# Attention with the softmax sums written by the exponentials, and k's bias on VectorE

## The chip, the cores and the metric

The kernel runs on one core of a Trainium2 chip. The metric is the device time of one execution in microseconds (us). The engines are named as in the profile: PE is TensorE (PEld its weight loads), ACT is ScalarE, DVE is VectorE, POOL is GpSimd, and SP issues the DMAs.

## The reference

Two layers run one after the other on x of shape 128 x 128 x 32 x 32 in float32. The first is attention over the batch at each of the 1024 pixels; the second is a Mamba block, which the change leaves as it is. The first layer, cut to what matters:

```python
xs  = x.reshape(B, C, L).transpose(2, 0, 1)            # L=1024 pixels, B=128, C=128
qkv = xs @ in_proj_weight.T + in_proj_bias
q, k, v = split(qkv, 3);  q = q * hd ** -0.5           # 4 heads of hd=32
scores = einsum('lhbd,lhed->lhbe', q, k)
attn = softmax(scores, axis=-1)                        # rows of 128
out  = einsum('lhbe,lhed->lhbd', attn, v).reshape(L, B, E)
y    = out @ out_proj_weight.T + out_proj_bias + xs
y    = layernorm(y) * norm_weight + norm_bias
```

## The kernel before, in words

`attention_layer` works on groups of four pixels (LG = 4), 256 groups in all; a group's tiles are 128 x 512. The layer's result goes to `mid` in DRAM, from which `mamba_layer` reads afterwards. Channels or batch lie on the partitions.

The work of a group is a list of tasks, each on one engine. `Plan` gives each task a time, its entry in `A_AT` plus the group's number times `A_PERIOD`, sorts the tasks of all groups by that time, and issues them in that order. Each engine so has one fixed queue in which tasks of up to six groups stand between one another, and it takes them strictly in turn. The waits between engines are added from the tiles and the PSUM banks that the instructions touch; the times themselves are in no instruction.

A group's tasks are these, with their lines:

- `picked` (L294, POOL) copies the group's columns of x to `xg`.
- `q_mm`, `k_mm` (L303, PE) project; `q_out` (L322, DVE) adds q's bias and scales by the negative of the scale, `k_out` (L329, ACT) adds k's bias. `v_mm` (L336, PE) and `v_out` (L348, DVE) do v, whose bias is put in later.
- The softmax is made in two halves f = 0, 1 of two pixels each. `scores0/1` (L363, PE) write the half's scores into `s_ps`, which has one PSUM bank for each head; each bank holds all four pixels of its head, so both halves lie in the same four banks. `top0/1` (L394, DVE) take each row's minimum, since the scores are negated. `exps00, exps01, exps10, exps11` (L373, ACT), one for each pixel, are four exponentials of 128 x 128 each, with the row's `top` as a bias read from SBUF.
- `summed0/1` (L385, POOL) add the upper half of each exponentials' row to the lower, twice, from 128 to 32 columns; `inverse0/1` (L410 and L411, DVE) sum these 32 and take the reciprocal; `shares0/1` (L417, DVE) multiply the half's 128 x 1024 exponentials by it.
- For each pixel, `turned0..3` (L435, PE) transpose its four heads, `kept0..3` (L443 on ACT, L441 on DVE for pixel 2) bring them to SBUF, `weighted0..3` (L447, PE) multiply by v. `o_out` (L477, DVE) brings the sum to SBUF.
- `residual` and `projected` (L486, L489, PE), `squared` (L500, ACT), `variance` (L507, PE), `rstd` (L492, L493, ACT) and `normed` (L515, DVE) make the output projection and the layernorm; `placed` (L522, POOL) scales and stores into the tile that SP writes out.

Of the kernel before, what the change touches and what calls it, by code (L numbers as in the profile page):

```python
# [11 lines left out]
AF = mybir.ActivationFunctionType  # L12
ALU = mybir.AluOpType
AX = mybir.AxisListType
# [3 lines left out]
P = 128  # L18
NB = 128
# [8 lines left out]
NH = 4  # L28
# [35 lines left out]
class Plan:  # L64
# [9 lines left out]
    def add(self, *args, **more):  # L74
        t = Task(*args, **more)
        t.image, t.place = self.image, len(self.tasks)
        t.at = t.image * self.period + self.times[t.name]
        deps = list(t.after)
        for k in t.reads:
            if k in self.wrote:  # L80
                deps.append(self.wrote[k])
        for k in t.writes:
            deps += self.read.get(k, ())
            if k in self.wrote:
                deps.append(self.wrote[k])
        for k in t.reads:
            self.read.setdefault(k, []).append(t)
        for k in t.writes:
            self.wrote[k], self.read[k] = t, []
        for x in deps:  # L90
            assert (x.at, x.place) < (t.at, t.place) or x is t, (x.name, t.name)
        self.tasks.append(t)
        return t
# [87 lines left out]
NE = 3  # L181
NET = 6
NSQ = 2
NARROW = 32
EVICT = (2,)
O_DVE = True
PARTS = 12
A_PERIOD = 10.33
A_AT = {
    "exps00": 22.9, "exps01": 21.02, "exps10": 17.58, "exps11": 18.7, "inverse0": 30.84,  # L190
    "inverse1": 25.62, "k_mm": 1.98, "k_out": 3.52, "kept0": 40.48, "kept1": 37.14, "kept2": 41.9,
    "kept3": 41.08, "load": 0.01, "normed": 58.45, "o_out": 48.87, "part": 16.16, "picked": 0.0,
    "placed": 59.65, "projected": 51.66, "q_mm": 6.66, "q_out": 8.24, "residual": 50.11,
    "rstd": 56.14, "scores0": 16.16, "scores1": 14.5, "shares0": 32.27, "shares1": 34.23,
    "squared": 53.2, "store": 59.66, "summed0": 24.57, "summed1": 21.75, "top0": 19.29,
    "top1": 15.91, "turned0": 39.2, "turned1": 35.99, "turned2": 40.75, "turned3": 38.62,
    "v_mm": 31.97, "v_out": 33.54, "variance": 54.6, "weighted0": 45.24, "weighted1": 46.07,
    "weighted2": 46.9, "weighted3": 47.73,
}


# [1 line left out]
def attention_layer(ctx: ExitStack, tc: tile.TileContext, ident, eps, x, w, mid, prepare):  # L203

    nc = tc.nc
# [7 lines left out]
    bqkv = const.tile([P, 3], F32, name="bqkv")  # L213
# [29 lines left out]
    def several(n, shape, name, pool=keep):  # L243
        return [pool.tile(shape, F32, name=f"{name}{j}") for j in range(n)]
# [3 lines left out]
    HL = LG // 2  # L248
# [7 lines left out]
    eTs = several(NET, [P, NH * NB], "eT")  # L256
    oTs = several(2, [P, GB], "oT")
    tops = several(2, [P, HL, NH], "top")
    halves = several(2, [P, HL, NH, NB // 2], "halved")
    sums = several(2, [P, HL, NH], "total")  # L260
    sqs = several(NSQ, [P, GB], "sq")
    s_ps = psum.tile([P, NH, LG, NB], F32, name="s_ps")
    plan = Plan(several(4, [P, GB], "m_ps", psum), A_PERIOD, A_AT)
    add = plan.add
# [5 lines left out]
    def heads(h):  # L270
        return slice(h * HD, (h + 1) * HD)
# [13 lines left out]
    def group(g):  # L285
        plan.image = g
        xg, qT, kT, v = xgs[g % NXG], qTs[g % NQK], kTs[g % NQK], vs[g % NV]
# [7 lines left out]
            writes=[kx],  # L295
        )

        def project(j, name, engine, move, key):
# [26 lines left out]
        project(  # L325
            1,
            "k",
            "ACT",
            lambda b: nc.scalar.activation(kT, b, AF.Identity, bias=bqkv[:, 1:2]),  # L329
            kk,  # L330
        )
        bank = Bank()
# [1 line left out]
        def v_mm(bank=bank):  # L334
# [14 lines left out]
            writes=[kv],  # L349
# [3 lines left out]

        def softmax(f):
            e, ke = es[f][g % NE], f"e{f}{g % NE}"
            ls = slice(f * HL, (f + 1) * HL)
            got = s_ps[:, :, ls, :].rearrange("p h l k -> p l h k")

            def scores():
                for i in range(f * HL, (f + 1) * HL):  # L360
                    cs = slice(i * NB, (i + 1) * NB)
                    for h in range(NH):
                        nc.tensor.matmul(  # L363
                            s_ps[:, h, i, :],
                            lhsT=qT[heads(h), cs],
                            rhs=kT[heads(h), cs],
                            start=True,
                            stop=True,
                        )

            def exps(i):
                for h in range(NH):
                    nc.scalar.activation(  # L373
                        e[:, i, h, :],
                        s_ps[:, h, f * HL + i, :],
                        AF.Exp,
                        bias=tops[f][:, i, h : h + 1],
                        scale=-1.0,
                    )

            def summed():
                src, w = e, NB // 2
                while w >= NARROW:
                    dst = halves[f][:, :, :, 0:w]
                    nc.gpsimd.tensor_tensor(  # L385
                        dst, src[:, :, :, 0:w], src[:, :, :, w : 2 * w], ALU.add
                    )
                    src, w = dst, w // 2

            add(f"scores{f}", "PE", scores, reads=[kq, kk], writes=[f"s{f}0", f"s{f}1"])  # L390
            add(
                f"top{f}",
                "DVE",
                lambda: nc.vector.tensor_reduce(tops[f], got, AX.X, ALU.min),  # L394
                reads=[f"s{f}0", f"s{f}1"],
                writes=[f"top{f}"],
            )
            for i in range(HL):
                add(
                    f"exps{f}{i}",  # L400
                    "ACT",
                    lambda i=i: exps(i),
                    reads=[f"s{f}{i}", f"top{f}"],
                    writes=[f"{ke}{i}"],
                )
            both = [f"{ke}{i}" for i in range(HL)]
            add(f"summed{f}", "POOL", summed, reads=both, writes=[f"half{f}"])

            def inverse():
                nc.vector.reduce_sum(sums[f], halves[f][:, :, :, 0:NARROW], AX.X)  # L410
                nc.vector.reciprocal(sums[f], sums[f])  # L411

            add(f"inverse{f}", "DVE", inverse, reads=[f"half{f}"], writes=[f"sum{f}"])
            add(
                f"shares{f}",
                "DVE",
                lambda: nc.vector.tensor_tensor(  # L417
                    e, e, sums[f].unsqueeze(3).to_broadcast([P, HL, NH, NB]), ALU.mult
                ),
                reads=[f"sum{f}"],  # L420
                writes=both,
            )

        for f in range(2):
            softmax(f)

        pv = Bank()
        for i in range(LG):
            f = i // HL
# [15 lines left out]
            def weighted(i=i, r=r):  # L445
# [16 lines left out]
                writes=[f"eT{r}"],  # L462
# [7 lines left out]
                reads=[f"eT{r}", kv],  # L470
# [4 lines left out]
            "o_out",  # L475
            "DVE" if O_DVE else "ACT",
            lambda: (nc.vector.tensor_copy if O_DVE else nc.scalar.copy)(oT, pv.tile),  # L477
            writes=[ko],
# [12 lines left out]
        def rstd():  # L491
# [9 lines left out]
            writes=[kz],  # L501
# [6 lines left out]
            reads=[kz],  # L508
# [7 lines left out]
            writes=[kz],  # L516
# [13 lines left out]
            reads=[kz],  # L530
# [10 lines left out]
    for g in range(NT):  # L541
        if g % PER == 0:
            b = g // PER
            plan.image = g - PER - 1 if b else -2
            if plan.image < 0:
                plan.image = b - 3
            add("load", "SP", lambda b=b: load(b))
        group(g)
        if 4 <= g < 4 + PARTS:
            add("part", "PE", prepare_part, take=[spare], give=[spare])  # L550
        if g % PER == PER - 1:
            add("store", "SP", lambda b=g // PER: store(b))
# [984 lines left out]
@with_exitstack  # L1537
def both_layers(ctx: ExitStack, tc: tile.TileContext, x, w, out):
    nc = tc.nc
    const = ctx.enter_context(tc.tile_pool(name="const", bufs=1))  # L1540
    dram = ctx.enter_context(
        tc.tile_pool(name="dram", bufs=1, space=bass.MemoryType.DRAM)
    )
    ident = const.tile([P, P], F32, name="ident")
    make_identity(nc, ident)
    eps = const.tile([P, 1], F32, name="eps")
    nc.vector.memset(eps, LN_EPS)
    mid = dram.tile([NB, P, L], F32, name="mid")
    b_const = ctx.enter_context(tc.tile_pool(name="b_const", bufs=1))
    with tc.tile_pool(name="b_prep", bufs=1) as prep:  # L1550
        constants = attention_layer(
            tc,
            ident,
            eps,
            x,
            w,
            mid,
            lambda bank: mamba_constants(tc, ident, eps, w, b_const, prep, bank),
        )
    mamba_layer(tc, ident, eps, mid, constants, out)  # L1560
# [50 lines left out]
```

## Time and profile before

| | |
|---|---|
| median of 3 runs | 15083.57 us (15081.0 to 15085.92) |
| the profiled execution | 15083.06 us, its span 15081.2 us |
| busy shares of the span | PE 88%, DVE 94%, ACT 82%, POOL 91% |
| attention layer | from the start to about 2888 us; 256 groups |
| a group in the steady state | about 10.97 us |
| granted TensorE clock, steady attention | 1.00 |

A group of instructions is read as: line, engine, operation, output and input tiles, shapes and count; then the busy time in us and the mean duration of one in ns; then the engine's idle time ahead of it and who ended that. In the timeline each row has the start in us, the length in us, then the instruction and, in brackets, the idle time just before it with its releaser.

### The profile page before, as it was taken

How to read it: one execution, taken by the hardware profiler on the slowest of the kernel's cores; microseconds unless marked ns; L12 is line 12 of the kernel's file. 1: busy time of each engine (PE TensorE's matmuls, PEld its weight loads, DVE VectorE, ACT ScalarE, POOL GpSimd, SP SyncE). 2: the span in 40 equal slices, each digit the busy share in tenths (PEclk: the TensorE clock that was granted, in tenths of full speed). 3: DMA queues.
4: the chain of work that ended last, by engine and by line, in shares of the span. 5: the costliest groups of instructions: out<-in, count | busy, mean ns of one | idle time of the engine just before them, and what ended most of it. 6: DMA issues, size and time to landing. Idle time of an engine off the chain costs nothing. (4 is left out here: it accounts for less than half of the span.)

```text
span 15081.2 us, 218873 instructions
## 1 busy us (share of the span) xinstructions
PE 13259.9 (88%) x78902; PEld 6352.1 (42%) x78902; DVE 14172.1 (94%) x9777; ACT 12324.6 (82%) x22790; POOL 13799.0 (91%) x5385
## 2 busy tenths in 40 slices
PE   8999999888888888888888888888888888888887
PEld 4555555433333333333333333333333333333333
DVE  7888888699999999999999999999999999999999
ACT  6777777688888888888888888888888888888887
POOL 6777777599999999999999999999999999999999
PEclk9999999999999999999999999999999999999999
DMA  2222222266666666666666666666666666666665
GB/s 50 57 46 51 52 46 46 56 168 169 168 169 168 168 170 169 169 169 169 168 169 169 169 169 169 169 169 169 168 169 170 168 169 168 168 169 169 170 168 146
DMA packets 1191586, 2180.31 MB, mean 145 GB/s; under 512 B 673232, under 2 KB 674272, under 8 KB 1190496
## 3 DMA queue, kind: packets, MB, share of 16 engines
q1 hardware_dynamic: 1190496, 2166.31, 59.5%
q8 instruction: 619, 10.14, 0.3%
q14 instruction: 471, 3.86, 0.1%
HBM read 1746.30 MB, written 419.43 MB: 144 GB/s over the span
## 5 line engine op out<-in xcount | busy, mean ns | idle before, releaser
L1338 POOL TENSOR_TENSOR dbu<-dtxr,brep 128x2048 f32<-128x2048 f32 x1280 | 5804.1, 4551 | 26.3 <-DMA dtxr<-dtxd 13.1
L1384 POOL TENSOR_TENSOR hc<-hc,crep 128x1024 f32<-128x1024 f32 x2304 | 5412.4, 2373 | 307.4 <-PE da L1331 205.3
L1363 ACT ACTIVATE da<-dtr,aneg 128x1024 f32<-128x1024 f32 x2560 | 2951.2, 1161 | 524.3 <-DVE hc L1384 502.1
L1376 DVE TENSOR_TENSOR_SCAN hc<-da,dbu 128x1024 f32<-128x1024 f32 x1408 | 3161.8, 2276 | 98.0 <-ACT da L1363 91.9
L1277 ACT ACTIVATE bx<-p_ps,bT 128x128 f32<-128x128 f32 (+1 forms) x8192 | 2791.4, 484 | 132.1 <-PE p_ps L1269 132.1
L1376 DVE TENSOR_TENSOR_SCAN da<-da,dbu 128x1024 f32<-128x1024 f32 x1152 | 2621.9, 2286 | 101.9 <-ACT da L1363 93.9
L1331 PE MATMUL da<-ident,bx 128*128 128x128 f32 x12288 | 1827.7, 294 | 501.8 <-DVE hc L1376 418.7
L1384 DVE TENSOR_TENSOR hc<-da,crep 128x1024 f32<-128x1024 f32 x1792 | 2161.8, 1218 | 47.8 <-PE y_ps L1403 7.5
L891 PE MATMUL p_ps<-tn,wk 128*128 128x512 f32 x4096 | 1987.3, 608 | 249.3 <-DVE tn L855 156.5
L1331 PEld LDWEIGHTS da<-ident,bx 128*128 128x128 f32 x12288 | 1488.4, 150 | 1635.4 <-DVE hc L1376 1074.0
L1363 ACT ACTIVATE dbu<-dtr,aneg 128x1024 f32<-128x1024 f32 x1536 | 1731.9, 1217 | 452.9 <-DMA dtr<-dtd 449.9
L1376 DVE TENSOR_TENSOR_SCAN hc<-dbu,da 128x1024 f32<-128x1024 f32 x896 | 1999.4, 2267 | 27.5 <-ACT dbu L1363 24.2
L1403 PE MATMUL y_ps<-hc,fold 128*32 128x512 f32 x16384 | 1972.9, 599 | 43.3 <-POOL hc L1384 30.4
L1376 DVE TENSOR_TENSOR_SCAN da<-dbu,da 128x1024 f32<-128x1024 f32 x640 | 1449.7, 2281 | 188.8 <-PE da L1331 126.4
L373 ACT ACTIVATE e<-s_ps,top 128x128 f32<-128x128 f32 x4096 | 1147.7, 384 | 338.4 <-PE s_ps L363 299.1
L952 PE MATMUL p_ps<-xpad,dwd 64*64 64x512 f32 x9216 | 1154.4, 593 | 111.0 <-ACT xm L923 103.6
L891 PEld LDWEIGHTS p_ps<-tn,wk 128*128 128x128 f32 x4096 | 709.9, 191 | 1148.8 <-issue 774.5
L1403 PEld LDWEIGHTS y_ps<-hc,fold 128*32 128x32 f32 x16384 | 475.5, 109 | 1188.6 <-issue 846.0
L385 POOL TENSOR_TENSOR halved<-e 128x512 f32<-128x512 f32 x512 | 916.3, 1790 | 25.6 <-ACT e L373 19.8
L417 DVE TENSOR_TENSOR e<-e,total 128x1024 f32<-128x1024 f32 x512 | 833.1, 1627 | 0.0
L294 POOL COPY xg<-xt 128x512 f32<-128x512 f32 x256 | 273.6, 1069 | 533.1 <-PE m_ps L486 496.6
L952 PEld LDWEIGHTS p_ps<-xpad,dwd 64*64 64x64 f32 x9216 | 362.6, 133 | 801.3 <-issue 569.2
(128 smaller groups left out, 19118.0 us busy)
## 6 DMA issues: line engine op xcount, KB each, us to landing
dtxr<-dtxd SPq DMA_DIRECT2D x2048, 256.0 KB, 5.4
dtr<-dtd SPq DMA_DIRECT2D x2048, 256.0 KB, 5.4
crep<-bcd SPq DMA_DIRECT2D x2048, 128.0 KB, 6.3
brep<-bcd SPq DMA_DIRECT2D x1536, 128.0 KB, 4.9
x<-mid SPq DMA_DIRECT2D x256, 512.0 KB, 5.5
dtd<-dtt SPq DMA_DIRECT2D x256, 512.0 KB, 5.1
dtxd<-dtt SPq DMA_DIRECT2D x256, 512.0 KB, 4.3
xt<-in_x SPq DMA_DIRECT2D x64, 1024.0 KB, 11.0
```

Of the source, the lines that this page charges most:

```text
L373: nc.scalar.activation(e[:, i, h, :], s_ps[:, h, f * HL + i, :], AF.Exp, bias=tops[f][:, i, h : h + 1], scale=-1.0,)
L385: nc.gpsimd.tensor_tensor(dst, src[:, :, :, 0:w], src[:, :, :, w : 2 * w], ALU.add)
L417: lambda: nc.vector.tensor_tensor(e, e, sums[f].unsqueeze(3).to_broadcast([P, HL, NH, NB]), ALU.mult),
L891: nc.tensor.matmul(a.tile, lhsT=wk[:, k, h * P : (h + 1) * P], rhs=tn[:, c * CH + k : (c + 1) * CH + k], start=k == 0, stop=c > 0 and k == ...
L952: nc.tensor.matmul(pair[r] .tile[c * HP : (c + 1) * HP] .rearrange("p (r q) -> p r q", q=HH), lhsT=dwd[rs, k, :], rhs=xpad[rs, y0 : y0 + r ...
L1277: nc.scalar.activation(bx[:, tb, ks, n, :], src, AF.Copy, scale=bT[:, j : j + 1])
L1331: nc.tensor.transpose(ps[:, tb * P : (tb + 1) * P], bx[:, tb, TENSOR[h, nb] * NDB + db].rearrange("p n d -> p (n d)"), ident,)
L1338: nc.gpsimd.tensor_mul(dbu[u // 2 % NDBU], dtxr[db // 2], brep[nb - 1].unsqueeze(1).to_broadcast([P, 2, L]),)
L1363: lambda: nc.scalar.activation(a, dtr[db // 2][:, db % 2, :], AF.Exp, scale=aneg[:, h * NDB + db, nb : nb + 1],),
L1376: lambda: nc.vector.tensor_tensor_scan(dst, a, b, 0.0, ALU.mult, ALU.add),
L1384: lambda: engine.tensor_mul(hc[u % 8], dst, crep[nb]),
L1403: nc.tensor.matmul(y_ps[db * GD : (db + 1) * GD, chunk(c)], lhsT=fold, rhs=hc[(i * NG + k) % 8][:, chunk(c)], start=False, stop=last,)
```

## The change

Each exponential now also has `accum_out`, which writes the sum of its row into `total`; the sums have three buffers for each half instead of one. The two POOL additions of each half and the DVE reduction are gone, and the reciprocal stands at the head of `shares`. `k_out` moves from ACT to DVE, as an addition with the bias read from SBUF. The times in `A_AT`, and so the order of every engine's queue, are new; `A_PERIOD` stays 10.33.

```diff
-NARROW = 32
+K_DVE = True
 A_AT = {
...
-    halves = several(2, [P, HL, NH, NB // 2], "halved")
-    sums = several(2, [P, HL, NH], "total")
+    sums = [several(NE, [P, HL, NH], f"total{f}_") for f in range(2)]
...
             "k",
-            "ACT",
-            lambda b: nc.scalar.activation(kT, b, AF.Identity, bias=bqkv[:, 1:2]),
+            "DVE" if K_DVE else "ACT",
+            lambda b: (
+                nc.vector.tensor_scalar(kT, b, bqkv[:, 1:2], None, ALU.add)
+                if K_DVE
+                else nc.scalar.activation(kT, b, AF.Identity, bias=bqkv[:, 1:2])
+            ),
...
                         bias=tops[f][:, i, h : h + 1],
                         scale=-1.0,
+                        accum_out=total[:, i, h : h + 1],
...
-            def summed():
-                src, w = e, NB // 2
-                while w >= NARROW:
-                    dst = halves[f][:, :, :, 0:w]
-                    nc.gpsimd.tensor_tensor(
-                        dst, src[:, :, :, 0:w], src[:, :, :, w : 2 * w], ALU.add
-                    )
-                    src, w = dst, w // 2
...
-            def inverse():
-                nc.vector.reduce_sum(sums[f], halves[f][:, :, :, 0:NARROW], AX.X)
-                nc.vector.reciprocal(sums[f], sums[f])
...
+            def shares():
+                nc.vector.reciprocal(total, total)
+                nc.vector.tensor_tensor(
+                    e, e, total.unsqueeze(3).to_broadcast([P, HL, NH, NB]), ALU.mult
+                )
```

In the steady state the queues of the two programs stand as follows (a group's worth, by task names):

| engine | before | after |
|---|---|---|
| ACT | exps01, squared, exps00, k_out, rstd, kept1, exps10, exps11, kept0, kept3 | exps00, kept0, kept1, exps01, kept3, squared, exps10, exps11, rstd |
| DVE | shares0, v_out, shares1, inverse1, top1, normed, o_out, q_out, top0, inverse0, kept2 | top1, shares0, v_out, q_out, top0, o_out, k_out, normed, shares1, kept2 |
| POOL | summed0, summed1, placed, picked | placed, picked |
| PE | k_mm, variance, weighted, scores1, weighted, turned, weighted, scores0, weighted, q_mm, turned twice, residual, turned, projected, v_mm | weighted, projected, v_mm, weighted, q_mm, scores0, weighted, variance, weighted, k_mm, scores1, turned twice, residual, turned twice |

## The prediction

> **What bounds it now.** First the busy shares, then two stretches of the attention layer, where the whole change lies.
>
> ```profile
> PE 13259.9 (88%) x78902; PEld 6352.1 (42%) x78902; DVE 14172.1 (94%) x9777; ACT 12324.6 (82%) x22790; POOL 13799.0 (91%) x5385
> ```
>
> ```profile
> 600.00:900.00 300.00, 278.02 (x2668) 165.75 (x2666) 269.40 (x357) 234.04 (x632) 222.00 (x165) 1.00 0.22 43
> 2400.00:2700.00 300.00, 278.02 (x2666) 165.70 (x2665) 269.40 (x357) 234.01 (x632) 222.24 (x165) 1.00 0.16 29
> ```
>
> The page's shares mix two layers; the windows (length, then busy PE, PEld, DVE, ACT, POOL, then the clock) show attention as a machine that repeats itself: PE 93%, DVE 90%, ACT 78%, POOL 74%, clock 1.00. No engine is full. One group takes 10.97 us (the same row in the timeline comes back 10.97 later), so something goes round in a circle of waits. The timeline of one group shows it:
>
> ```profile
> 1500.19 1.23 DVE L394 TENSOR_REDUCE top<-s_ps 128x8 f32<-128x1024 f32 x1
> 1500.24 1.07 ACT L443 COPY eT<-m_ps 128x512 f32<-128x512 f32 x2
> ...
> 1501.45 1.14 ACT L373 ACTIVATE e<-s_ps,top 128x128 f32<-128x128 f32 x4
> ...
> 1502.17 1.25 POOL L385 TENSOR_TENSOR halved<-e 128x512 f32<-128x512 f32 x1
> ...
> 1502.46 2.06 DVE L417 TENSOR_TENSOR e<-e,total 128x1024 f32<-128x1024 f32 x1
> ...
> 1505.04 1.21 DVE L417 TENSOR_TENSOR e<-e,total 128x1024 f32<-128x1024 f32 x1
> ...
> 1506.92 1.18 DVE L394 TENSOR_REDUCE top<-s_ps 128x8 f32<-128x1024 f32 x1
> ...
> 1508.03 0.74 DVE L515 SCALAR_TENSOR_TENSOR sq<-m_ps,by,sq 128x512 f32<-128x512 f32 x1
> ...
> 1508.16 0.73 PE L363 MATMUL s_ps<-kT,qT 32*128 32x128 f32 x16 [0.61 <-DVE top L394]
> ...
> 1508.88 1.24 POOL L522 TENSOR_SCALAR yt<-sq,nw,nb 128x512 f32<-128x512 f32 x1 [0.70 <-DVE sq L515]
> 1508.96 2.18 ACT L373 ACTIVATE e<-s_ps,top 128x128 f32<-128x128 f32 x8 [1.14 <-PE s_ps L363]
> ...
> 1510.34 0.75 DVE L322 TENSOR_SCALAR qT<-m_ps,bqkv 128x512 f32<-128x512 f32 x1 [0.34 <-PE m_ps L303]
> ```
>
> DVE works without a gap from one q_out to the end of top1 (1499.37, one period before 1510.34, to 1508.10: 8.73 us). Then PE does scores0, weighted and q_mm until q_out can start at 1510.34: 2.24. Together 10.97, the period. Two things inside it matter. The first `shares` takes 2.06 where the second takes 1.21: a POOL addition had started 0.29 earlier. And the eight exponentials wait for scores0 (1508.16 to 1508.89), though they read the other half: both halves lie in the same banks, and PE, DVE and ACT take these banks in turn.
>
> **Part by part.** *POOL additions* (L385, 4 for each group): POOL keeps picked and placed, 2.3 us of 10.97. POOL is not in the circle, so its own time is worth nothing; what counts is that shares0 falls from 2.06 to 1.21, -0.85. *Reductions* (L410, 0.41 each): two leave DVE, -0.66 by start-to-start (0.41 less the 0.08 by which DVE's successors overlap). *k's bias*: ACT loses 0.69 (L329); DVE gains an instruction like q_out, 0.75 less 0.08 = +0.67. kT is read by the scores of its group some 7 us later, so a late k_out costs nothing beyond its place in DVE's queue. DVE's sum so falls by about 0.84; the old circle would take 10.13 by that, but its order is gone and a new one must be looked for.
>
> *Reads of the sums.* The built program has 4096 instructions on ACT of a kind that was not there, one for each exponential; I take them for the reads of the sums. No row shows one. Call x what each adds. Its neighbours, from ACT's timeline in the second layer and at the start:
>
> ```profile
> 5031.58 0.27 ACT L1167 COPY bT<-p_ps 128x32 f32<-128x32 f32 x2 [0.76 <-PE p_ps L1162]
> ```
>
> ```profile
> 88.86 0.20 ACT L619 ACTIVATE bns<-bns 128x1 f32<-128x1 f32 x1
> ```
>
> Two small copies, one right behind the other, take 0.27; one alone is 0.189 (L1167's median), so the second costs 0.08. Consecutive exponentials start 0.25 apart though each lasts 0.38: they overlap by 0.13. A read that must see its exponential finished loses that, and the 128x1 row standing alone takes 0.20: at worst 0.33. At best 0, if it hides behind the next one's fetch of its bias; below 0 is excluded, since an instruction more in a queue taken in turn shortens nothing. I take 0.09, nearest to the small copy that follows its like, a little over because it needs its predecessor's result.
>
> *The Trainium skill's price.* "ScalarE: Activation LUTs", section "What ACT_TABLE_LOAD costs", gives 186 ns plus 0.833 per element and an overlap of 93, so a one-element instruction would be about 94 ns as an estimate; no row here has it.
>
> **What goes round after.** In the new order ACT does exps10, then PE scores0 (which waits for ACT), then ACT exps11 (which waits for PE), then DVE top0 (waits for ACT), and every turn changes engine. (These waits stand in the built program; the banks again, and top0's place behind exps11.) Handovers are from the timeline above: DVE to PE 0.05 (1508.10, 1508.16), PE to ACT 0.07 (1508.89, 1508.96), DVE to ACT 0.03 (1501.42, 1501.45), ACT to DVE 0.03 (the last exponential ahead of 1500.19 ends at 1500.16). ACT to PE has no row; 0.05, between the others. Four exponentials in a row are 1.15 (1.14 to 1.17).
>
> Circle B, the banks alone: top1 1.18+.03, exps10 1.15+.05, scores0 0.73+.07, exps11 1.15+.03, top0 1.23+.05, scores1 0.73+.07, then exps00, kept0, kept1, exps01 in ACT's queue 1.02+0.48+0.48+1.15, and .03 back to top1: 9.63, and 16 reads: 9.63+16x.
>
> Circle A leaves ACT at top0 and goes on along DVE's queue: top1 through exps11 as above 4.39 with 8 reads; top0 1.15, o_out 0.61, k_out 0.67, normed 0.66, reciprocal 0.24, shares1 1.13, kept2 0.56 (each from its start to the next one's, so its length less 0.08; the reciprocal's 0.24 has the 0.04 that L417 waits for it): 9.41+8x. But shares1 now stands behind normed, and placed, which normed releases on POOL, starts 0.11 after normed's end (1508.88 against 1508.77), shares1 0.16 after. If the POOL instruction that came first holds up the multiplication as the addition did (0.96 of it was left, 0.85 was lost), 1.19 is left here and 1.08 is lost: 10.49+8x. Bounds 0 and 1.08; below 0 is excluded, since shares1 at 1.13 is the free row. I take 1.08: it is the same DVE instruction, and POOL is first by 0.05.
>
> *A rule against the change here.* "SBUF — State Buffer", section "Who interferes with whom", says that a VectorE instruction with two SBUF inputs contends with a GpSimd one that reads SBUF, whichever starts first holding it to its end. Row and rule meet for additions; for a one-input POOL instruction no row shows it. By the rule circle A is 10.49+8x; were it only for additions, 9.41+8x.
>
> PE alone needs 0.927 of 10.97 = 10.17, a floor.
>
> **Sum.** x = 0.09: A 11.21, B 11.07. A sets the period: +0.24 on 256 groups = +61 us. The profiled execution took 15083.06 (span 15081.2 and 1.9 around it), 0.5 below the median: 15145. Break-even is x = 0.06 for A, 0.084 for B; so k's bias, 0.67 in A, and the reductions saved are both small against the order of turns and 8 or 16 reads. If A loses its collision, B is next at 11.07 (+26 us); the sign stays.
>
> **Rivals.** (1) *The read hides*: x at 0.055, which is the small copy's 0.08 without its 32 columns (0.83 ns each: a 512-column copy costs 0.48 behind its like, 1.07 for the two at 1500.24 less 0.59 for one). A 10.93 with the collision: -10 us; B 10.51 where shares1 goes first: -118 us, 14965. At x = 0 without collision PE's floor decides, 10.17: -205 us, 14878. For: ACT overlaps small instructions, 22% of ACT is idle, POOL gets out of DVE's way. Against: the circle has no slack, so each tenth of a us in x is 0.8 or 1.6 in the period. It decides below x = 0.06. (2) *The read waits for its exponential's end*: x = 0.20, B 12.83, +476 us, 15559; at 0.33, 14.91, +1009 us. For: rstd's second instruction, which needs the first's result, starts only 0.03 after its end, without overlap. Against: the sum is formed inside ACT, not read from memory, so no such wait need arise; no row tells. (3) *No reads*: the sums come free with the exponentials, x = 0; then it is rival 1's end. The extra instructions speak against it.
>
> **Numbers.** Forecast (x 0.07 to 0.13) 0.45; read hidden 0.35, of which most is faster and a part within 0.2%; read waiting 0.20. A measurement of this kernel tells about 0.2%, 30 us, from no change. Faster 0.30, same 0.12, slower 0.58. The range goes from rival 1 without collision (14960) to B at x = 0.18 (12.51, +394, and some for rival 2: 15500); out of it stay a hidden read at PE's floor, 0.07, and the waiting read's far end, 0.12.
>
> **What would show it.** Right: the period in the timeline near 11.2; four exponentials lasting about 1.5 with their reads; shares0 1.21, shares1 above 2 with placed starting just ahead of it; scores0 released by ACT; busy shares of about 91% for PE (10.17 of 11.21), 83% for ACT (8.58 less 0.69, 1.44 more), 30% for POOL, and DVE near its 90%, since the collision gives back what it saved. Wrong: reads of 0.05 or less between exponentials, shares1 at 1.21, or PE above 95% with ACT idle. If x is over 0.15, DVE waits long ahead of both tops, and ACT is the fullest engine.

## The result: 0.28% slower, by a circle through the score banks

The changed kernel takes 15124.22 us (median of ten, 15115.99 to 15131.28) against 15083.62 for the kernel before on the same chip, a ratio of 1.0028 (95% interval 1.0018 to 1.0037): 40.6 us more. The profiled execution has a span of 15118.3 us. A group now takes 11.126 us in the steady state, where it took 10.974; 0.152 more on 256 groups is 39 us. In the traces the last placed ends at 2887.6 us before and at 2925.4 after, 37.8 later, and the spans differ by 37.1, so the whole difference lies in the attention layer.

The window of the changed kernel that answers to the ones of before (length, then busy PE, PEld, DVE, ACT, POOL, the clock):

```profile
600.00:900.00 300.00, 289.86 (x2642) 161.59 (x2645) 239.75 (x325) 248.38 (x1026) 87.03 (x54) 1.00 0.22 43
```

VectorE fell from 90% to 80%, GpSimd from 74% to 29%, ScalarE rose from 78% to 83%: the change did take its work off the two engines it meant to relieve, and the kernel got slower. PE, at 97%, seems nearly full; run 1 below shows its own work in this order to be 10.61 of the 11.13.

The profile page's groups of the exponentials show how each of them now leaves two rows:

```profile
L376 ACT ACTIVATE e<-s_ps,top 128x128 f32<-128x128 f32 x4096 | 1457.9, 377 | 537.7 <-PE s_ps L366 476.7
...
L376 ACT ACTIVATION_READ_ACCUMULATOR e<-s_ps,top 128x1 f32 x4096 | 878.6, 215 | 0.0
```

The read of the sum is an instruction of its own, 0.215 us long. In the rows from 1501.25 on below, it starts before its exponential has ended (1501.51 against 1501.62), and the next exponential (1501.61) before the read has ended (1501.70), so its length is not its price: exponentials that follow one another start 0.250 us apart before (median of 3331) and 0.342 after, so a read costs 0.092.

The timeline of one group shows the circle. It is read by the brackets: each turn waits for the engine that had the banks last.

```profile
1500.45 0.73 PE L366 MATMUL s_ps<-kT,qT 32*128 32x128 f32 x16 [0.32 <-ACT e L376]
...
1501.25 0.37 ACT L376 ACTIVATE e<-s_ps,top 128x128 f32<-128x128 f32 x1 [0.85 <-PE s_ps L366]
...
1501.51 0.19 ACT L376 ACTIVATION_READ_ACCUMULATOR e<-s_ps,top 128x1 f32 x1
1501.61 0.36 ACT L376 ACTIVATE e<-s_ps,top 128x128 f32<-128x128 f32 x1
...
1502.78 1.23 DVE L389 TENSOR_REDUCE top<-s_ps 128x8 f32<-128x1024 f32 x1 [1.29 <-ACT e L376]
...
1504.06 0.54 PEld L366 LDWEIGHTS s_ps<-kT,qT 32*128 32x128 f32 x16 [0.89 <-DVE top L389]
1504.06 0.73 PE L366 MATMUL s_ps<-kT,qT 32*128 32x128 f32 x16
...
1504.86 0.37 ACT L376 ACTIVATE e<-s_ps,top 128x128 f32<-128x128 f32 x1 [0.82 <-PE s_ps L366]
...
1506.02 2.30 POOL L514 TENSOR_SCALAR yt<-sq,nw,nb 128x512 f32<-128x512 f32 x1 [7.90 <-DVE total L404]
1506.07 1.23 DVE L405 TENSOR_TENSOR e<-e,total 128x1024 f32<-128x1024 f32 x1
...
1508.47 0.26 ACT L376 ACTIVATION_READ_ACCUMULATOR e<-s_ps,top 128x1 f32 x1
...
1508.76 1.23 DVE L389 TENSOR_REDUCE top<-s_ps 128x8 f32<-128x1024 f32 x1 [0.87 <-ACT e L376]
...
1510.02 0.37 ACT L376 ACTIVATE e<-s_ps,top 128x128 f32<-128x128 f32 x1 [0.23 <-DVE top L389]
1510.13 1.22 DVE L405 TENSOR_TENSOR e<-e,total 128x1024 f32<-128x1024 f32 x1
```

scores0 (1500.45) waits for ACT's exps10, exps11 (1501.25) waits for PE, top0 (1502.78) for ACT, scores1 (1504.06, by its weight load) for DVE, exps00 (1504.86) for PE; two copies and exps01 run on to 1508.73, top1 (1508.76) waits for ACT, and the next exps10 (1510.02) for top1. At each of these turns the next engine starts within 0.07 us of the end of the one before. Where the three engines stand idle is seen in the list of waits between 1000 and 2033 us (total, times, longest), some 93 groups:

```profile
DVE top L389 <- ACT e L376: 201.2, 186, 1.3
ACT e L376 <- PE s_ps L366: 155.0, 186, 0.8
PEld s_ps L366 <- ACT e L376: 105.2, 92, 1.1
PEld s_ps L366 <- DVE top L389: 82.6, 93, 0.9
```

VectorE alone stands 2.2 us of each group waiting for exponentials. By this circle a relief of VectorE can't help, and whatever makes one of ScalarE's turns longer counts in full; runs 1 to 3 test it.

### The profile page after: what moved, and what is told of

Read it like the earlier page. It is cut to its first block, busy times and chain, and to the rows that moved or that the text cites. A ratio compares the mean times of both kernels' runs of the same rounds, so it can differ in the third digit from the quotient of the medians.

```text
span 15118.3 us, 221409 instructions
## 1 busy us (share of the span) xinstructions
PE 13405.2 (89%) x78902; PEld 6336.0 (42%) x78902; DVE 13936.1 (92%) x9521; ACT 12488.0 (83%) x26630; POOL 12544.5 (83%) x4361
## 3 DMA queue, kind: packets, MB, share of 16 engines
q8 instruction: 619, 10.14, 0.3%
## 5 line engine op out<-in xcount | busy, mean ns | idle before, releaser
L514 POOL TENSOR_SCALAR yt<-sq,nw,nb 128x512 f32<-128x512 f32 x256 | 585.7, 2288 | 2025.4 <-DVE total L404 1988.0
L376 ACT ACTIVATE e<-s_ps,top 128x128 f32<-128x128 f32 x4096 | 1457.9, 377 | 537.7 <-PE s_ps L366 476.7
L389 DVE TENSOR_REDUCE top<-s_ps 128x8 f32<-128x1024 f32 x512 | 627.1, 1225 | 545.6 <-ACT e L376 545.6
L376 ACT ACTIVATION_READ_ACCUMULATOR e<-s_ps,top 128x1 f32 x4096 | 878.6, 215 | 0.0
L1139 POOL TENSOR_TENSOR dtt<-dtt,xm 128x1024 f32<-128x1024 f32 x256 | 608.0, 2375 | 108.1 <-DMA dtd<-dtt 101.9
```

The lines of the kernel that those rows point to most:

```text
L376: nc.scalar.activation(e[:, i, h, :], s_ps[:, h, f * HL + i, :], AF.Exp, bias=tops[f][:, i, h : h + 1], scale=-1.0, accum_out=total[:, i, ...
L1139: lambda: nc.gpsimd.tensor_mul(dtt[h], dtt[h], im["xm"][h]),
```

## The experiments

Each comparison is with the kernel before on the same chip, which took 15099.62 us in the first four runs and 15088.38 in the second four. Against these, the changed kernel's 1.0028 stands for 15142 and 15131 us.

**1. No reads.** The exponentials write no sums, and `total` is set to 1 once.

```diff
+    for one in sums[0] + sums[1]:
+        nc.vector.memset(one, 1.0)
...
-                        accum_out=total[:, i, h : h + 1],
```

> The changed kernel without accum_out: the row sums are left out (each is held at 1), all else as in the changed kernel, the timetable too. Theory, the circle through the score banks: the period is 9.63 plus 16 reads of 0.093; without the reads the banks need 9.63, VectorE's queue 9.41, and PE's own work (about 10.2 to 10.4) sets the period, so 14890 to 14940 us, and PE is over 95% busy. Rival, the reads are hidden and the new order alone made the kernel slower: within 10 us of 15124.

Measured: 15002.04 us, ratio 0.9933 (0.9918 to 0.9948), the group 10.61 us. The window:

```profile
600.00:900.00 300.00, 300.00 (x2781) 169.31 (x2779) 255.87 (x339) 219.68 (x622) 90.26 (x56) 1.00 0.29 56
```

The reads cost 0.52 us for each group, 132 us by the period and 140 by the times: they are not hidden, and the rival falls. But the 98 us gained against before fall some 45 us short of the least that the theory gave. PE has not one gap (300.00 of 300.00). The ends of its rows are modelled, but the distances between its starts say the same: they are those of run 6, where one product alone waits for another engine. So PE's own work in this order is 10.61, not 10.2 to 10.4. What makes it so is tried in 7.

**2. Reads in one half.** `accum_out` is left out for f = 1, whose sums are held at 1.

```diff
+    for one in sums[1]:
+        nc.vector.memset(one, 1.0)
...
-                        accum_out=total[:, i, h : h + 1],
+                        accum_out=total[:, i, h : h + 1] if f == 0 else None,
```

> accum_out in the first half alone; the second half's row sums are left out (held at 1). Theory: 9.63 plus 8 reads of 0.093 is 10.38, near PE's own work, so 14925 to 14960 us. Rival, reads hidden: 15124. If each read cost twice as much where it ends a turn on the banks, 4 of them counting, it would be halfway between the others.

Measured: 15012.15 us, ratio 0.9941 (0.9924 to 0.9958), the group 10.63, PE again without a gap. Eight reads cost almost nothing (0.02 over none) and the other eight 0.50. That is what a circle of 9.63 plus 0.093 for each read gives beside PE's 10.61: 10.38 with eight, under it; 11.12 with sixteen, over it. The time came out some 35 us over the range given, again for PE's share.

**3. k's bias back on ScalarE**, in the new order.

```diff
-K_DVE = True
+K_DVE = False
```

> The changed kernel with k's bias back on ScalarE, at the same place in the timetable (ahead of exps00). Theory: on ScalarE k_out falls into the 0.8 us that it waits there for scores1, and VectorE's queue is not in the circle, so the period stays 11.13 and the time 15115 to 15135 us. Rival, VectorE's queue with normed, the multiplication and k_out sets the period: 0.67 less for each group, 14950 us.

Measured: 15138.74 us, ratio 1.0025 (1.0015 to 1.0035), the group 11.125 as with the change. VectorE is at 75% here and ScalarE at 89%, and nothing moves: neither queue is the bound, and this part of the change is worth nothing in this order.

**4. The sums by the exponentials, in the order of before.** All times of `A_AT` are before's (those of the tasks that are gone stand unused), and k's bias is on ScalarE.

```diff
-K_DVE = True
+K_DVE = False
...
 A_AT = {
-    "exps00": 17.78, "exps01": 20.59, "exps10": 23.43, "exps11": 24.93, "k_mm": 5.93,
...
+    "exps00": 22.9, "exps01": 21.02, "exps10": 17.58, "exps11": 18.7, "inverse0": 30.84,
...
```

> The sums by accum_out, but k's bias on ScalarE and every time from the table of before (so the old order without the POOL additions and VectorE's reductions). Theory, what counts is how often the turn on the banks changes engine and what stands between: in the old order the eight exponentials of the second half follow one another and only squared stands between the other two fours, so about 10.5 to 10.65 and 14965 to 15005 us, faster than before. Rival, 16 reads cost 1.5 in any order: the old circle's 10.97 less 0.85 and 0.66 plus 1.5 is 10.96, 15080 us.

Measured: 15022.69 us, ratio 0.9947 (0.9932 to 0.9962), the group 10.68, just over the 10.65 that was given. So the sums on ScalarE, all sixteen reads of them, make the kernel faster by 77 us in the old order. It is the new order that loses that and more: run 3, which differs from this one in the order alone, is 116 us slower. In the old order the eight exponentials of the second half stand in one run, and PE goes on with other work meanwhile; it waits about 0.2 for the banks here, by its starts.

**5. k's bias on VectorE, in the order of before**: run 4 with `K_DVE = True`.

> The sums by accum_out under the old times, and k's bias on VectorE as in the change, at its old time. Against the run with it on ScalarE (period 10.67) this tells what that part is worth: VectorE gets 0.67 more, and waits 0.3 to 0.5 ahead of three of its instructions, so it is partly hidden: 10.67 to 10.85, 15022 to 15070 us on a chip where the kernel before takes 15100. If VectorE's queue is in that circle in full, 11.3 and slower than before.

Measured: 15025.06 us, ratio 0.9960 (0.9946 to 0.9974), the group 10.74. The intervals of 4 and 5 overlap; by the periods this part costs 0.06 on each group, 15 us, of the 0.67 that VectorE gets. That its waits (2.2 us of each group in run 4) cover the rest is the likely reason, not a shown one.

**6. Shorter turns.** From the changed kernel, the two copies that stand between exps00 and exps01 go to VectorE, and two instructions move in their queues.

```diff
-EVICT = (2,)
+EVICT = (0, 1, 2)
...
-    "scores0": 14.21, "scores1": 17.23, "shares0": 22.86, "shares1": 29.43, "squared": 53.73,
+    "scores0": 14.21, "scores1": 17.23, "shares0": 22.86, "shares1": 35.7, "squared": 55.2,
```

> The changed kernel with kept0 and kept1 on VectorE (EVICT 0, 1, 2), shares1 moved in VectorE's queue to the wait ahead of top0, and squared moved behind exps10 in ScalarE's. All 16 reads stay. Theory, the circle through the banks: it loses the two copies between exps00 and exps01, 9.63 less 0.96 plus 16 reads is 10.17, below PE's own 10.61 in this order, so 10.61 to 10.7 and 14990 to 15025 us on a chip where the kernel before takes 15100, the same as without reads. Rival, reads cost their time on ScalarE wherever they stand: 11.1, 15140 there. Rival, VectorE with three more instructions becomes the bound: over 10.8.

Measured: 15031.17 us, ratio 0.9962 (0.9947 to 0.9977), the group 10.74, PE busy 298.32 of 300. With all the reads in place and VectorE loaded from 80% to 95%, the kernel is 0.39 us faster for each group than the changed one. The rivals of 11.1 and of VectorE as the bound fall. The period came out 0.04 over the range given: PE, though all but full, waits 0.13 of it ahead of scores1 for top0. Which circle makes it wait is seen in 7.

**7. PE's order.** In addition, weighted1 and weighted2 are moved next to weighted0 and weighted3.

```diff
-    "weighted0": 41.76, "weighted1": 43.98, "weighted2": 45.78, "weighted3": 47.0,
+    "weighted0": 41.76, "weighted1": 41.9, "weighted2": 46.9, "weighted3": 47.0,
```

> As the version with short turns, and weighted1 next to weighted0, weighted2 next to weighted3 in PE's queue, so that four fewer times PE goes between full 128-row products and the narrow ones of heads. If the 0.1 us that a 512-column product takes more next to a narrow one (1.13 against 1.02) is what makes PE's own time 10.61, PE needs about 10.2 to 10.25, the banks 10.17, and the period is 10.2 to 10.35: 14905 to 14945 us on a chip where the kernel before takes 15100. If these 0.1 are only a matter of how ends are drawn in the records, it stays at 10.61, 15010 us.

Measured: 14952.63 us, ratio 0.9909 (0.9894 to 0.9924), the group 10.405. This beats both kernels, by 136 us and about 178. The window, with VectorE and PE both at 98%:

```profile
600.00:900.00 300.00, 294.49 (x2829) 174.90 (x2826) 294.78 (x405) 235.81 (x1043) 63.70 (x58) 1.00 0.30 58
```

So PE's order is worth real time, and its starts show where. From scores1 to the next scores0 PE goes through its queue without a wait in both runs, in 7.13 us in run 6 and in 6.80 here; this 0.33 is the whole gain. Two weighted in one run take 0.57 from start to start instead of twice 0.36 (0.14 less), and v_mm and q_mm, each with a narrow neighbour less, are followed 0.09 and 0.10 sooner. The other pair of weighted, between scores0 and scores1, saves as much, but there PE only waits longer for top0. (PE goes between full and narrow products 8 times for each group here and 10 times in run 6; "four fewer" was miscounted.)

What a narrow neighbour costs a 512-column product is seen in the run without reads. Two of its rows, each with the one behind it, are:

```profile
1503.27 1.13 PE L500 MATMUL m_ps<-sq,a_mean 128*128 128x512 f32 x2
1504.32 0.42 PE L440 MATMUL m_ps<-eT,v 128*32 128x128 f32 x8
...
1507.32 1.02 PE L479 MATMUL m_ps<-xg,resc 128*128 128x512 f32 x2
1508.18 1.04 PE L428 MATMUL m_ps<-ident,e 128*128 128x128 f32 x8
```

Between narrow products the next instruction starts 1.05 after a 512-column one, between full ones 0.86, so each narrow neighbour costs it about 0.1. "TensorEngine Tiling (Array Packing)" in the Trainium skill, section "Key Properties", says that changing the tiling mode drains the engine. These rows agree with a cost at each change; that a drain is what costs, they don't tell.

The group came out 0.05 over the upper end that I gave, and the trace shows what keeps it there, a third circle:

```profile
1501.02 0.73 PE L366 MATMUL s_ps<-kT,qT 32*128 32x128 f32 x16
...
1501.81 0.37 ACT L376 ACTIVATE e<-s_ps,top 128x128 f32<-128x128 f32 x1 [0.53 <-PE s_ps L366]
...
1503.10 0.21 ACT L376 ACTIVATION_READ_ACCUMULATOR e<-s_ps,top 128x1 f32 x1
...
1503.35 1.23 DVE L389 TENSOR_REDUCE top<-s_ps 128x8 f32<-128x1024 f32 x1
...
1504.63 0.73 PE L366 MATMUL s_ps<-kT,qT 32*128 32x128 f32 x16 [0.20 <-DVE top L389]
...
1511.42 0.73 PE L366 MATMUL s_ps<-kT,qT 32*128 32x128 f32 x16
```

From scores0 (1501.02) the banks go to exps11, to top0, which starts 0.04 behind the last read, and back to PE for scores1 (1504.63): 3.61. Then PE's queue leads to the next scores0: 6.80. Together they are 10.41, and with run 6's 7.13 they are 10.74, its period. So in both runs PE's queue and one round of the banks set the period, and neither PE's own work nor VectorE's queue alone; four of the sixteen reads still lie in that round.

**8. Who holds whom up, GpSimd or VectorE.** In VectorE's queue normed goes ahead of k_out, so that placed starts well ahead of shares1.

```diff
-    "normed": 59.67, "o_out": 47.67, "part": 14.21, "picked": 0.0, "placed": 60.72,
+    "normed": 58.9, "o_out": 47.67, "part": 14.21, "picked": 0.0, "placed": 60.72,
```

> The changed kernel with normed ahead of k_out in VectorE's queue, so that placed starts on POOL about 0.7 us ahead of shares1 instead of 0.04. If the instruction that starts first keeps the other waiting, placed takes 1.24 as alone and shares1 is held up by about 0.5, to 1.65 to 1.75. If VectorE's multiplication goes first against a POOL instruction with one input whenever they meet, shares1 stays at 1.22 and placed grows to about 2.3. The period stays 11.13 either way, since VectorE's queue has 0.87 to spare ahead of top1: 15115 to 15140 us by the times of the first runs.

Measured: 15128.42 us, ratio 1.0029 (1.0018 to 1.0040), the group 11.126, as expected. The timeline:

```profile
1504.50 1.24 POOL L514 TENSOR_SCALAR yt<-sq,nw,nb 128x512 f32<-128x512 f32 x1 [8.05 <-DVE sq L507]
...
1505.20 1.43 DVE L405 TENSOR_TENSOR e<-e,total 128x1024 f32<-128x1024 f32 x1
...
1505.95 1.63 POOL L292 COPY xg<-xt 128x512 f32<-128x512 f32 x1 [0.21 <-PE m_ps L478]
```

placed, first by 0.70, takes its 1.24, and shares1 loses 0.21; the copy that starts behind shares1 takes 1.63 instead of 1.06. So the two hold each other up also where GpSimd has one input, the row that was missing, and the one that is clearly first goes on. But shares1 lost only 0.21 of the 0.54 that placed still had by its row, where I expected 0.5. "SBUF — State Buffer" in the Trainium skill, section "Who interferes with whom", calls the ports that the two share an exclusive lock; a hold to the recorded end of placed is more than this row shows.

## Why the prediction was right, and where it was not

- **The sign and the size.** 15145 was forecast, 15124 measured: +61 against +41 us. The range held it. That the sum came within 21 us is in part luck: it was the sum of circle A, which does not bound, as said below.
- **The price of a read.** 0.09 was taken, 0.092 is measured; it lies by the small copy that follows its like, far from the bound of 0.33. Rival 2, a read that waits for its exponential's end, falls. The estimate of 94 ns from "ScalarE: Activation LUTs" in the Trainium skill ("What ACT_TABLE_LOAD costs"), which no row of before had, agrees with these 92.
- **Circle B.** 9.63 + 16 x 0.093 is 11.12; measured 11.126. Its terms hold but for hundredths: exps00 to the end of exps01 3.87 (3.13 and eight reads are 3.87), four exponentials with their reads 1.50 (for 1.52), the handover from ACT to PE, of which there was no row, 0.05; top1 took 1.23 and not 1.18.
- **The step that failed: circle A's collision.** I had placed start first, hold up shares1 by 1.08, and so make A the longer circle at 11.21. In the trace placed does start first, by 0.04 (median of 189), but shares1 takes 1.23, as shares0 does with GpSimd idle, and placed is the one that is held up, to 2.30. A is then 9.41 + 8 x 0.093 = 10.15 and bounds nothing. Run 8 fits with a row of GpSimd that begins before and ends after the time in which it holds VectorE up, so that 0.04 between two starts would not decide; what exactly is held when, no run tells. (In the kernel before, the one addition that started 0.06 ahead of a multiplication did hold it up, to 2.29.) The sum stayed near because B stood just below A; for a lost collision +26 us was given. The measured +41 is B with a read of 0.092 to 0.093 instead of 0.09 (8 to 12 us more), and the hundredths of the other terms.
- **PE's floor.** 10.17 was PE's busy share of before, taken as if it went with the work alone. It goes with the order: 10.61 in the new one (run 1), and 10.14 by PE's starts, its wait left out, in run 7's. So rival 1's prices were too good: with a read that costs nothing the gain is 98 us, not 205, and not 118. PE's busy share, forecast at 91%, is 97% for that reason.
- **Busy shares.** ScalarE is at 83% as forecast; VectorE at 80% and not 90, since the collision did not fall on it. GpSimd's 29% meets the forecast 30 by luck: the two instructions that it keeps, 2.3 us by the prediction's own figure, would be 21% of 11.21, and it is at 29% because placed was the one held up, to 2.30.
- **k's bias.** Said to be small; shown as nothing in the new order; about 15 us in the old one, by the periods.

What the change lost is thus shown: not by the sums on ScalarE, which gain 77 us in the old order, but by an order in which ScalarE, PE and VectorE take the score banks in turn so that ScalarE has three turns in a group, two of four exponentials and one of eight with two copies between them, and the reads on top. Taking the circle apart, with banks of its own for each half, was not tried.

## What to carry to other kernels

When no engine is full, look for what all of them take in turn (here four banks that hold both halves of the scores) and sum the circle around it, handovers included: an instruction added inside costs in full, one taken from an engine outside it is worth nothing, until the next circle or a full engine is reached. An instruction's price is what it adds between the starts of its neighbours, not its length. A busy share of another order is no floor: what PE needs depends on what stands next to what.

## What the runs showed of the hardware that I had not expected

- A 512-column float32 product (two rows in the trace) takes 1.13 us behind products of 32 rows or 32 columns and 1.02 behind full ones; with narrow ones on both sides it costs 0.2 us more from start to start. Sixteen narrow products in one run take 0.57 where two runs of eight take 0.71. Moving two tasks to join such runs gave 0.33 us for each group.
- A GpSimd instruction whose row starts 0.04 us ahead of that of VectorE's multiplication was held up by it for 1.06 us; first by 0.70, it held VectorE up for only 0.21 of the 0.54 it still had.
- Reads of the accumulator get longer along an unbroken stretch of ScalarE's work, from 0.19 to 0.26 us, and the distance between exponentials stays 0.34.
